# Two mixing steps with joined rows, moved from first and second to fifth and sixth place

## The chip, the cores and the metric

The kernel runs on one core of one Trainium2 chip, in one launch. The metric is the device time in microseconds (us). The profile is of one execution on that core; its engines are PE (matmul; PEld is the load of its weights), DVE (vector), ACT (scalar), POOL (GpSimd) and SP, which here only issues DMAs. Each engine works through its own queue of instructions in order.

## The reference

Four layers act on x of 4 images, 64 channels and 256 x 256 points. Layers 0, 2 and 3 are long convolutions with filters that a small network makes, separable in the two directions, plus x times a bias. Layer 1 is the one that concerns us: a two-dimensional Haar transform, for each of two filters a product with v, a mix of the 64 channels, a soft threshold, and the inverse transform of the sum.

```
f1 = haar2d(x)
acc = jnp.zeros_like(f1[:, :conv_w.shape[1]])
for i in range(v.shape[0]):
    f3 = f1 * v[i]
    f4 = jnp.einsum('bchw,oc->bohw', f3, conv_w[i])
    f5 = jnp.sign(f4) * jax.nn.relu(jnp.abs(f4) - tau[i])
    acc = acc + f5
y = haar2d(acc, inverse=True)
return y + x
```

## The kernel before

The four images are two groups of two. A *tile* of work is one group and one round (2 of the 64 channels); there are 32 rounds in a group. The convolutions are matmuls with Toeplitz matrices in float32.

**Phase A** (rows, columns, residual, then the forward Haar levels) goes through 64 tiles. Each has ten *pieces* j = 0 to 9, calls that record a few instructions: rows on PE with ACT copying the result (ay, L444), columns on PE with DVE adding the residual (x1, L464), sixteen forward steps on POOL (L344 and L346; the largest stand in pieces 0 and 1), the last Haar product on PE (a3ps, L308) with DVE scaling it (L477), and stores of the coefficients into the DRAM tensor coef of the group.

**Phase B** (`phase_b(grp)`, once for each group) mixes channels. It has 64 *steps* s; a step is four rows of points, with all 64 channels of the group's images on the partitions. Each step has two *units*, u = 2s and 2s + 1, one for each filter; so 128 units, of three pieces (u, 0), (u, 1), (u, 2). For one unit:

- `mix` (L607): eight matmuls of 64 x 64 into f4, which has one PSUM buffer; issued in the piece (u - 1, 1)
- `multiply` in (u, 0), DVE L626: x = f4 * v. `sign` in (u, 1), ACT L632: m. `magnitude` in (u, 2), ACT L641
- `less` in (u + 1, 0), DVE L646, and `threshold` in (u + 1, 1), DVE L651: subtract tau, cut at zero, times m
- `add` in (u + 2, 0), POOL L669 and L670 (first filter: plus the old coefficients f and `other`) or L666 (second filter), into gt
- `exchange` in (2s, 2), ACT L657: the tile `other`, a copy of half of f across the partitions
- `store` of gt into the DRAM tensor mixed, `load_f` and `load_v` for later steps, all on SP

Buffers in rings: ft 4, v 3, raw 3, m 3, gt 3, other 2, x 2, f4 1. A new tile takes the buffer of the tile so many places back, and its writer waits for the last reader of that one.

In group 1 (the last) the second filter of most steps is not thresholded here: DVE copies f4 to a tile raw (L623), which is stored in the DRAM tensor unshrunk, and phase C does the threshold later. Only the two *held* steps, those with the rows of the coarsest level, are done in full in phase B; for them the tile raw holds v and tau of the second filter, and zeros are stored in unshrunk (a memset on POOL, L681).

The forward transform leaves the coarsest level of the held steps unfinished: their rows have to be joined before mixing and parted after it. `join` (L575 to L586) is eight DVE operations on 64 x 256 for each of two images, in place in the two ft tiles, with a spare tile taken from the ring m; `part` (L588 to L599) is eight POOL operations on 64 x 512, in place in the two gt tiles, also with a spare from the ring m. The held steps are the first two, s = 0 and 1. All of join is one piece right ahead of `mix(0)`; all of part stands in the piece (6, 0), followed by the stores of both steps:

```
            if i == 0 and s == 3:
                part()
                store(0)
                store(1)
```

**Phase C** does the inverse transform and the last two convolutions for 64 tiles of 18 pieces: scales on ACT (L362), sixteen inverse steps on POOL (L385; the last two write ci) or DVE for the first two tiles (L387), the product c0ps on PE (L308), which reads ci and is copied to z by ACT or DVE (L849), then c1r, c1c, c2r, c2c on PE (L296) with their copies (ACT L861) and residuals (DVE L880), and stores of out. It reads the DRAM tensors mixed and unshrunk. Filters are loaded on SP (toep, L158), parts of g too (L758).

**The order** is written out by hand: `beside(main, side, lead, tail)` (L963) puts the pieces of side evenly between the pieces of main, and the instructions are recorded in that order for all engines. Phase B of group 0 runs beside the second half of phase A, about 1.5 side pieces to a main piece. Phase B of group 1 runs beside the first half of phase C, 0.8 side pieces to a main piece. In each, 13 pieces go ahead of piece (0, 0): `start` (which issues four `load_f` and three `load_v`), ten that do nothing, join, and `mix(0)`.

Of the kernel before, what the change touches and what calls it, by code (L numbers as in the profile page):

```python
# [41 lines left out]
F32 = mybir.dt.float32  # L42
AF = mybir.ActivationFunctionType
ALU = mybir.AluOpType
# [3 lines left out]
P = 128  # L48
B, C, N = 4, 64, 256
# [16 lines left out]
GROUPS = 2  # L66
NB = B // GROUPS
# [3 lines left out]
PAD = 128  # L71
# [2 lines left out]
HALVES = 2 * ROUNDS  # L74
STEPS = C
FULL = 2

A_PIECES = 2 * BLOCKS + 2
C_PIECES = 4 * BLOCKS + 2
# [2 lines left out]
W = 2 * N  # L82
# [16 lines left out]
def conv_haar_kernel(  # L99
    ctx: ExitStack, tc: tile.TileContext, x, zT, w1, wbd, cols, wo, decay, wo_first, decay_first, bias, forward, inverse, wrow, pack, v, v_rows, out  # L100
):
    nc = tc.nc
# [186 lines left out]
    def half(r):  # L289
        return slice(r * ROW, (r + 1) * ROW)  # L290
# [113 lines left out]
    def run(ops, count):  # L404
        for _ in range(count):
            next(ops, None)
# [117 lines left out]
    def phase_b(grp):  # L524

        units = 2 * STEPS
        mixers = []

        def raw(u):
            return grp == GROUPS - 1 and u % 2 == 1 and FULL <= u // 2 < STEPS  # L530
        st = [dict() for _ in range(STEPS)]
        un = [dict() for _ in range(units)]
        pieces = []

        def step_of(ap, s, images):

            n = NB * W
# [12 lines left out]
        def load_v(s):  # L550
            if s >= STEPS:
                return
            d = st[s]
            d["v"], d["tau"] = [], []

            def fetch(first, count, tag):
                n = 2 * count * W
                t = bp.tile([P, count, 2, W], F32, tag=tag, name=f"{tag}_{grp}_{first}_{s}", bufs=3)
                at = v.offset + s * P * (4 * W + PAD) + first * 2 * W
                rows = bass.AP(v.tensor, at, [[4 * W + PAD, P], [1, n]])  # L560
                nc.sync.dma_start(t.rearrange("p i k w -> p (i k w)"), rows)
                d["v"] += [t[:, i, 0] for i in range(count)]
                d["tau"] += [t[:, i, 1] for i in range(count)]
# [5 lines left out]
        def four(name, at, b):  # L569

            tiles = [st[s][name] for s in range(2)]
            tiles.append(bp.tile([P, NB, W], F32, tag="m", name=f"spare_{name}_{grp}_{b}", bufs=3))
            return [t[at, b, bass.ts(h, N)] for t in tiles for h in range(2)]

        def join(image):  # L575

            a, b, c, d, t, u = four("f", half(image), image)
            op = nc.vector.tensor_tensor
            op(t, a, b, ALU.add)
            op(b, a, b, ALU.subtract)  # L580
            op(u, c, d, ALU.add)
            op(d, c, d, ALU.subtract)
            nc.vector.tensor_scalar(c, b, math.sqrt(2.0), None, ALU.mult)
            nc.vector.tensor_scalar(d, d, math.sqrt(2.0), None, ALU.mult)
            op(a, t, u, ALU.add)
            op(b, t, u, ALU.subtract)  # L586

        def part():  # L588

            a, b, c, d, t, u = four("g", half(0), slice(0, NB))  # L590
            op = nc.gpsimd.tensor_tensor
            op(t, a, b, ALU.add)
            op(b, a, b, ALU.subtract)
            nc.gpsimd.tensor_scalar(u, c, math.sqrt(2.0), None, ALU.mult)
            op(a, t, u, ALU.add)
            nc.gpsimd.tensor_scalar(d, d, math.sqrt(2.0), None, ALU.mult)
            op(c, b, d, ALU.add)
            op(d, b, d, ALU.subtract)
            op(b, t, u, ALU.subtract)  # L599

        def mix(u):
            s, i = divmod(u, 2)
            un[u]["f4"] = bps.tile([P, NB, W], F32, tag="f4", name=f"f4_{grp}_{u}", bufs=1)
            for b in range(NB):
                for r in range(2):
                    q = r ^ b
                    nc.tensor.matmul(  # L607
                        un[u]["f4"][half(q), b, :],
                        mixers[0][half(r), bass.ts(i, C)],
                        st[s]["f"][half(r), b],  # L610
                        start=True,
                        stop=True,
                        tile_position=(r * ROW, q * ROW),
                    )
# [5 lines left out]
        def multiply(u):  # L620
            if raw(u):
                t = st[u // 2]["raw"] = bp.tile([P, NB, W], F32, tag="raw", name=f"raw_{grp}_{u}", bufs=3)
                nc.vector.tensor_copy(t, un[u]["f4"])  # L623
                return
            un[u]["x"] = bp.tile([P, NB, W], F32, tag="x", name=f"x_{grp}_{u}", bufs=2)
            nc.vector.tensor_tensor(un[u]["x"], un[u]["f4"], both(u, "v"), ALU.mult)  # L626

        def sign(u):
            if raw(u):
                return  # L630
            un[u]["m"] = bp.tile([P, NB, W], F32, tag="m", name=f"m_{grp}_{u}", bufs=3)
            nc.scalar.activation(un[u]["m"], un[u]["x"], AF.Sign)  # L632
# [20 lines left out]
        def exchange(s):  # L653

            st[s]["other"] = bp.tile([P, W], F32, tag="other", name=f"other_{grp}_{s}", bufs=2)
            for q in range(2):
                nc.scalar.copy(st[s]["other"][half(q)], st[s]["f"][half(1 - q), 1])  # L657

        def add(u):
            s, i = divmod(u, 2)  # L660
            if raw(u):
                un[u].clear()
                return
            m = un[u]["m"]
            if i:
                nc.gpsimd.tensor_tensor(st[s]["g"], st[s]["g"], m, ALU.add)  # L666
            else:
                g = st[s]["g"] = bp.tile([P, NB, W], F32, tag="gt", name=f"gt_{grp}_{s}", bufs=3)
                nc.gpsimd.tensor_tensor(g[:, 0], m[:, 0], st[s]["f"][:, 0], ALU.add)  # L669
                nc.gpsimd.tensor_tensor(g[:, 1], m[:, 1], st[s]["other"], ALU.add)  # L670
            un[u].clear()

        def store(s):
            to, g = step_of(mixed[grp], s, st[s]["g"])
            nc.sync.dma_start(to, g)
            st[s].clear()

        def store_raw(s):
            if s < FULL:
                t = st[s]["raw"] = bp.tile([P, NB, W], F32, tag="raw", name=f"none_{grp}_{s}", bufs=3)  # L680
                nc.gpsimd.memset(t, 0.0)  # L681
            to, g = step_of(unshrunk, s, st[s]["raw"])
# [301 lines left out]
    bp = pool("b", 2, during)  # L984
# [4 lines left out]
    a = a[-2 * A_PIECES :]  # L989
# [7 lines left out]
    bp = pool("b2", 2, during)  # L997
# [132 lines left out]
```

## Time and profile before

| what | us |
|---|---|
| median of three runs | 2571.49 |
| lowest, highest | 2568.22, 2571.54 |
| the profiled execution | 2557.88 |
| its span, first to last instruction | 2556.1 |
| PE busy in the span | 2314.9 (91%) |
| POOL busy | 2075.5 (81%) |
| DVE busy | 1835.7 (72%) |
| ACT busy | 1324.5 (52%) |

The shares are means over phases that differ. Group 0's mixing starts at about 429 us of the span (its first join operation), group 1's at 1133; the last multiply of group 1 is at 1841.5. In the page's 40 slices each slice is 63.9 us. In a line of the timeline the first number is the start, the second the time, and the bracket tells how long the engine had stood idle and which instruction released it. A line that begins with SPq is the issue of a DMA, not its transfer.

The operations that the change moves, from the answers for single lines (four executions of each line of join, two of each of part):

| line | engine | operation | ns min / median / max |
|---|---|---|---|
| L579 | DVE | tensor_tensor 64x256 | 422 / 441 / 593 |
| L581 | DVE | tensor_tensor 64x256 | 419 / 422 / 2556 |
| L583 | DVE | tensor_scalar 64x256 | 284 / 292 / 336 |
| L593 | POOL | tensor_tensor 64x512 | 1263 / 1270 / 1276 |
| L594 | POOL | tensor_scalar 64x512 | 1489 in both groups |
| L666 | POOL | add of the second filter | 2347 / 2362 / 2377 |
| L681 | POOL | memset | 943 / 948 / 954 |

### The profile page before, as it was taken

The page shows a single profiled execution, that of the slowest core. Times are in us where ns is not written, and L with a number is a line of the kernel's source. Part 1 is how long each engine was busy: PE and PEld are TensorE (multiplying, and loading weights), DVE is VectorE, ACT ScalarE, POOL GpSimd, SP SyncE. Part 2 cuts the span into 40 slices and gives each one's busy share as a digit, 9 for nine tenths or more (in the row PEclk, how much of TensorE's full clock was granted, in tenths as well). Part 3 has the DMA queues.
Part 4 walks back from the last instruction along what each step waited for, and adds up shares of the span by engine and source line. Part 5 has one row for each costly group of instructions (what it writes and reads, how often), then busy time and mean ns, then how long its engine had stood idle before and what let it go on. Part 6 is the DMA issues. An engine that isn't in the chain of part 4 may idle for free.

```text
span 2556.1 us, 118462 instructions
## 1 busy us (share of the span) xinstructions
PE 2314.9 (91%) x53292; PEld 1788.5 (70%) x53292; DVE 1835.7 (72%) x2049; ACT 1324.5 (52%) x2187; POOL 2075.5 (81%) x2428
## 2 busy tenths in 40 slices
PE   5999998788888888867999999999999999999999
PEld 4887787444444444646777877677788888888887
DVE  2555545799999999756677777767767777777763
ACT  1221212566666666325666666666656556556552
POOL 1898887889999999868768776766879999999990
PEclk8999999899999999989999999999999999999999
DMA  7676898699999999755989998889876666666643
GB/s 212 222 239 233 294 313 299 241 347 322 336 342 317 345 335 317 260 182 205 320 309 334 325 328 306 305 297 317 291 227 225 217 208 223 211 209 219 221 159 110
DMA packets 203677, 685.25 MB, mean 268 GB/s; under 512 B 29289, under 2 KB 30826, under 8 KB 190755
## 3 DMA queue, kind: packets, MB, share of 16 engines
q1 hardware_dynamic: 203171, 677.67, 77.3%
q8 instruction: 419, 6.86, 1.1%
q14 instruction: 87, 0.71, 0.1%
HBM read 427.93 MB, written 249.63 MB: 265 GB/s over the span
## 4 chain that ended last, share of the span: by engine, by line
PE 45%; DVE 5%; DMA 2%; issue 2%; ACT 2%; POOL 1%; SPq 0%; DVEq 0%; ACTq 0%; POOLq 0%
PE c2c L296 10%; PE c2r L296 10%; PE c1r L296 9%; PE c1c L296 8%; PE f L607 4%; PE c0ps L308 4%; DVE m L651 1%; DVE cy L880 1%; DVE x L646 1%; DVE x L626 1%; DMA g<-mixed 1%; ACT ch L861 0%; DMA toep<-filt 0%; DMA ft<-coef 0%; DMA rows<-in_v_rows 0%
## 5 line engine op out<-in xcount | busy, mean ns | idle before, releaser
L385 POOL TENSOR_TENSOR i<-i,g 128x16 f32<-128x16 f32 x744 | 437.3, 608 | 27.2
L296 PEld LDWEIGHTS a2ps<-toep,ay 64*64 64x64 f32 x8192 | 304.4, 136 | 143.4 <-DVE f L477 71.9
L607 PE MATMUL f<-ft,mix 64*64 64x512 f32 x2048 | 297.2, 619 | 117.7 <-DVE x L626 95.7
L296 PE MATMUL a2ps<-toep,ay 64*64 64x128 f32 (+3 forms) x8192 | 354.7, 305 | 30.5 <-DVE f L477 28.7
L296 PE MATMUL a1ps<-toep,x 64*64 64x64 f32 (+3 forms) x8192 | 340.7, 302 | 15.6 <-DMA x<-in_x 12.2
L296 PEld LDWEIGHTS a1ps<-toep,x 64*64 64x64 f32 x8192 | 292.1, 135 | 88.2 <-issue 43.2
L296 PEld LDWEIGHTS c2c<-toep,ch 64*64 64x64 f32 x8192 | 279.5, 134 | 72.5 <-issue 36.9
L296 PEld LDWEIGHTS c1c<-toep,ch 64*64 64x64 f32 x8192 | 275.9, 133 | 69.5 <-issue 38.3
L296 PE MATMUL c1r<-toep,z 64*64 64x64 f32 (+3 forms) x8192 | 309.8, 299 | 14.9 <-issue 9.9
L385 POOL TENSOR_TENSOR ci<-i,g 128x1024 f32<-128x1024 f32 x124 | 317.0, 2577 | 4.6
L296 PEld LDWEIGHTS c1r<-toep,z 64*64 64x64 f32 x8192 | 275.2, 135 | 60.7 <-issue 25.8
L444 ACT COPY ay<-a1ps 128x512 f32<-128x512 f32 x256 | 137.3, 589 | 347.0 <-PE a1ps L296 346.4
L632 ACT ACTIVATE m<-x 128x1024 f32<-128x1024 f32 x194 | 206.0, 1062 | 212.2 <-DVE x L626 104.5
L669 POOL TENSOR_TENSOR gt<-m,ft 128x512 f32<-128x512 f32 x128 | 163.4, 1277 | 181.1 <-DVE m L651 177.5
L296 PE MATMUL c2c<-toep,ch 64*64 64x128 f32 (+3 forms) x8192 | 306.7, 298 | 3.1 <-ACT ch L861 1.8
L296 PE MATMUL c2r<-toep,cy 64*64 64x192 f32 (+3 forms) x8192 | 302.8, 297 | 3.0 <-DMA toep<-filt 2.0
L296 PE MATMUL c1c<-toep,ch 64*64 64x128 f32 (+3 forms) x8192 | 301.0, 297 | 2.8 <-issue 2.8
L296 PEld LDWEIGHTS c2r<-toep,cy 64*64 64x64 f32 x8192 | 271.0, 134 | 46.0 <-issue 17.8
L861 ACT COPY ch<-c2r 128x512 f32<-128x512 f32 x256 | 137.4, 591 | 280.3 <-PE c2r L296 279.5
L477 DVE TENSOR_TENSOR f<-a3ps,wrow_sb 128x512 f32<-128x512 f32 x256 | 161.5, 682 | 133.0 <-PE a3ps L308 133.0
L626 DVE TENSOR_TENSOR x<-f,v 128x1024 f32<-128x1024 f32 x192 | 233.5, 1216 | 15.7 <-PE f L607 15.3
L880 DVE SCALAR_TENSOR_TENSOR o<-cy,bias_sb,c2c 128x512 f32<-128x512 f32 x256 | 176.7, 742 | 90.6 <-PE c2c L296 88.7
(84 smaller groups left out, 3917.6 us busy)
## 6 DMA issues: line engine op xcount, KB each, us to landing
toep<-filt SPq DMA_DIRECT2D x384, 224.0 KB, 5.3
ft<-coef SPq DMA_DIRECT2D x128, 512.0 KB, 7.5
v<-in_v SPq DMA_DIRECT2D x64, 1024.0 KB, 10.3
mixed<-gt SPq DMA_DIRECT2D x128, 512.0 KB, 6.8
g<-mixed SPq DMA_DIRECT2D x256, 256.0 KB, 5.2
x<-in_x SPq DMA_DIRECT2D x128, 256.0 KB, 4.4
coef<-f SPq DMA_DIRECT2D x128, 256.0 KB, 3.9
x<-in_x SPq DMA_DIRECT2D x32, 1024.0 KB, 8.3
```

The source lines that it names most:

```text
L296: nc.tensor.matmul(ps[r][half(c), j % 2, k * ROW :], data[half(r), c, k, bass.ts(j, ROW)], t(r, c)[:, : N - k * ROW], start=k == 0, stop=k ...
L308: nc.tensor.matmul(ps[r][half(c)].rearrange("p h k -> p (h k)"), matrix[half(r)], pairs(r, c).rearrange("p h k -> p (h k)"), start=True, s ...
L385: engine.tensor_tensor(to, s, d, op)
L444: later(lambda y=y, ps=ps: nc.scalar.copy(y, ps))
L477: later(lambda f=f, ps=ps, w=w: nc.vector.tensor_tensor(f, ps, w, ALU.mult))
L607: nc.tensor.matmul(un[u]["f4"][half(q), b, :], mixers[0][half(r), bass.ts(i, C)], st[s]["f"][half(r), b], start=True, stop=True, tile_posi ...
L626: nc.vector.tensor_tensor(un[u]["x"], un[u]["f4"], both(u, "v"), ALU.mult)
L632: nc.scalar.activation(un[u]["m"], un[u]["x"], AF.Sign)
L646: nc.vector.tensor_tensor(un[u]["a"], un[u]["a"], both(u, "tau"), ALU.subtract)
L669: nc.gpsimd.tensor_tensor(g[:, 0], m[:, 0], st[s]["f"][:, 0], ALU.add)
L861: later(lambda y=y, ps=ps: nc.scalar.copy(y, ps))
L880: nc.vector.scalar_tensor_tensor(to, of, bias_sb[:, at : at + 1], ps, ALU.mult, ALU.add)
```

## The change

The steps get an `order`: places 0 to 3 take the steps 2 to 5, places 4 and 5 the held steps 0 and 1, and from place 6 on each step is where it was. The kernel's s is now a place; `step_of` and the load of v look the step up.

- The piece of join is replaced by one that does nothing; it is still 13 pieces to piece (0, 0).
- join is a generator, four operations after each of the pieces (6, 0), (6, 1), (6, 2), (7, 0). Both images share a spare of one row, taken from the ring other instead of m.
- part is a generator, two operations after each of (13, 1), (13, 2), (14, 0), (14, 1). Its spare is from the ring m. The two stores come after (14, 2).
- The stores of the other early steps are no longer held back: in group 0 the places 0 to 3 are stored like later ones.
- In group 1 the units 1 and 3 become raw copies, and the units 9 and 11 get the full work of the second filter. The rows v and tau for it are loaded after (7, 2) and (9, 2) instead of with the first load_v. The memsets for unshrunk move along.

```diff
+LATE = 4
...
+        order = [*range(FULL, FULL + LATE), *range(FULL), *range(FULL + LATE, STEPS)]
+        held = range(LATE, LATE + FULL)
 
         def raw(u):
-            return grp == GROUPS - 1 and u % 2 == 1 and FULL <= u // 2 < STEPS
+            return grp == GROUPS - 1 and u % 2 == 1 and 0 < u < units and u // 2 not in held
...
-            fetch(0, 2 if grp < GROUPS - 1 else 1, "v")
-            if grp == GROUPS - 1 and not raw(2 * s + 1):
-                fetch(1, 1, "raw")
...
+        def join():
+
+            spare = bp.tile([P, 1, W], F32, tag="other", name=f"spare_f_{grp}", bufs=2)
             op = nc.vector.tensor_tensor
-            op(t, a, b, ALU.add)
...
+            for image in range(NB):
+                a, b, c, d, t, u = four("f", half(image), image, spare)
+                yield op(t, a, b, ALU.add)
...
         def part():
 
-            a, b, c, d, t, u = four("g", half(0), slice(0, NB))
+            spare = bp.tile([P, NB, W], F32, tag="m", name=f"spare_g_{grp}", bufs=3)
+            a, b, c, d, t, u = four("g", half(0), slice(0, NB), spare)
...
         def store_raw(s):
-            if s < FULL:
+            if s in held:
...
-                if i == 0 and s == 3:
-                    part()
-                    store(0)
-                    store(1)
-                if i == 0 and s > 3 and not raw(2 * s - 3):
+                if i == 0 and s > 1 and s - 2 not in held and not raw(2 * s - 3):
                     store(s - 2)
...
+                if i and s + 1 in held and grp == GROUPS - 1:
+                    fetch(s + 1, 1, 1, "raw")
+            if u == 2 * LATE - 2 and j == 0:
+                joining.append(join())
+            if u // 2 == LATE - 1:
+                run(joining[0], 4)
+            at = 3 * (u - 2 * (LATE + FULL) - 1) + j - 1
+            if at == 0:
+                joining.append(part())
+            if 0 <= at < 4:
+                run(joining[1], 2)
+            if at == 4:
+                for k in held:
+                    store(k)
...
-        pieces += [start] + [lambda: None] * 10 + [lambda: [join(b) for b in range(NB)], lambda: mix(0)]
+        joining = []
+        pieces += [start] + [lambda: None] * 11 + [lambda: mix(0)]
```

More of the change, by code (lines that the diff above doesn't have):

```diff
@@ L535, in step_of @@
         def step_of(ap, s, images):
-            n = NB * W
+            n, s = NB * W, order[s]
             at = ap.offset + s // 2 * PAIR + s % 2 * P // CI * n
@@ L552, in load_v @@
                 return
[L553 to L563, printed above, removed]
@@ L565, in load_v @@
-            fetch(0, 2 if grp < GROUPS - 1 else 1, "v")
-            if grp == GROUPS - 1 and not raw(2 * s + 1):
-                fetch(1, 1, "raw")
[L569 to L577, printed above, removed]
-            op = nc.vector.tensor_tensor
[L579 to L586, printed above, removed]
+            st[s]["v"], st[s]["tau"] = [], []
@@ new lines, in load_v, with fetch @@
+            fetch(s, 0, 2 if grp < GROUPS - 1 else 1, "v")
+        def fetch(s, first, count, tag):
+            d, n = st[s], 2 * count * W
+            t = bp.tile([P, count, 2, W], F32, tag=tag, name=f"{tag}_{grp}_{first}_{s}", bufs=3)
+            at = v.offset + order[s] * P * (4 * W + PAD) + first * 2 * W
+            rows = bass.AP(v.tensor, at, [[4 * W + PAD, P], [1, n]])
+            nc.sync.dma_start(t.rearrange("p i k w -> p (i k w)"), rows)
+            d["v"] += [t[:, i, 0] for i in range(count)]
+            d["tau"] += [t[:, i, 1] for i in range(count)]
@@ new lines, in four @@
+        def four(name, at, b, spare):
+            rows = [(st[s][name], b) for s in held] + [(spare, slice(0, spare.shape[1]) if b == slice(0, NB) else 0)]
+            return [t[at, b, bass.ts(h, N)] for t, b in rows for h in range(2)]
+        def join():
+            spare = bp.tile([P, 1, W], F32, tag="other", name=f"spare_f_{grp}", bufs=2)
+            op = nc.vector.tensor_tensor
+            for image in range(NB):
+                a, b, c, d, t, u = four("f", half(image), image, spare)
+                yield op(t, a, b, ALU.add)
+                yield op(b, a, b, ALU.subtract)
+                yield op(u, c, d, ALU.add)
+                yield op(d, c, d, ALU.subtract)
+                yield nc.vector.tensor_scalar(c, b, math.sqrt(2.0), None, ALU.mult)
+                yield nc.vector.tensor_scalar(d, d, math.sqrt(2.0), None, ALU.mult)
+                yield op(a, t, u, ALU.add)
+                yield op(b, t, u, ALU.subtract)
@@ L588, in part @@
         def part():
-            a, b, c, d, t, u = four("g", half(0), slice(0, NB))
+            spare = bp.tile([P, NB, W], F32, tag="m", name=f"spare_g_{grp}", bufs=3)
+            a, b, c, d, t, u = four("g", half(0), slice(0, NB), spare)
             op = nc.gpsimd.tensor_tensor
[L592 to L596, printed above, removed]
@@ L597, in part @@
-            op(c, b, d, ALU.add)
-            op(d, b, d, ALU.subtract)
-            op(b, t, u, ALU.subtract)
+            yield op(t, a, b, ALU.add)
+            yield op(b, a, b, ALU.subtract)
+            yield nc.gpsimd.tensor_scalar(u, c, math.sqrt(2.0), None, ALU.mult)
+            yield op(a, t, u, ALU.add)
+            yield nc.gpsimd.tensor_scalar(d, d, math.sqrt(2.0), None, ALU.mult)
+            yield op(c, b, d, ALU.add)
+            yield op(d, b, d, ALU.subtract)
+            yield op(b, t, u, ALU.subtract)
```

## The prediction

> **What bounds the kernel now.** I read the cores first (one core, clock 0.981), then a table of stretches chosen from the page's 40 slices, then the order of time around both starts of the mixing, and the chain of waits for the second. All times are of the profiled execution. It took 2557.88 us, 1.78 of it outside its span of 2556.1; the median of the three runs is 2571.49, so I forecast a difference and put it on both.
>
> ```profile
> core 0: us, PE busy (x) PEld busy (x) DVE busy (x) ACT busy (x) POOL busy (x), PEclk, DMA share, GB/s
> 463.00:497.80 34.80, 21.02 (x314) 13.98 (x312) 22.61 (x24) 14.74 (x18) 31.89 (x32) 0.85 0.46 164
> 497.80:521.30 23.50, 20.17 (x314) 12.93 (x312) 22.55 (x24) 15.88 (x20) 21.31 (x23) 0.93 1.02 410
> 521.30:1000.00 478.70, 388.20 (x6326) 228.45 (x6324) 457.67 (x466) 311.57 (x388) 434.94 (x477) 0.99 0.94 333
> 1130.00:1150.00 20.00, 9.95 (x93) 4.70 (x87) 10.02 (x17) 5.47 (x9) 7.13 (x6) 0.66 1.00 337
> 1150.00:1193.00 43.00, 39.84 (x958) 32.83 (x950) 35.92 (x32) 29.83 (x51) 35.68 (x29) 1.00 0.47 158
> 1193.00:1203.50 10.50, 0.47 (x8) 0.00 (x0) 3.42 (x2) 3.63 (x6) 10.34 (x7) 0.72 0.66 227
> 1300.00:1800.00 500.00, 473.13 (x11143) 388.47 (x11138) 362.79 (x345) 319.88 (x557) 368.75 (x410) 0.99 0.92 317
> ```
>
> Two regimes. Beside phase A (group 0, to about 1000) DVE sets the pace: 457.67 of 478.70 us, 96%, with POOL at 91%. Beside phase C (group 1) it is PE, 95%. A tile of phase A takes 23.5 us; the one from 463.0 takes 34.8 with the same DVE work, so it lost 11.3. PE did almost nothing from 1193 to 1203.5. Both holes are at part.
>
> ```profile
> 437.11 1.23 DVE L626 TENSOR_TENSOR x<-f,v 128x1024 f32<-128x1024 f32 x1 [2.06 <-PE f L607]
> 472.64 1.06 ACT L632 ACTIVATE m<-x 128x1024 f32<-128x1024 f32 x1 [6.47 <-POOL gt L670]
> 483.49 1.06 ACT L632 ACTIVATE m<-x 128x1024 f32<-128x1024 f32 x1 [6.50 <-POOL gt L599]
> ...
> 512.33 2.38 POOL L666 TENSOR_TENSOR gt<-gt,m 128x1024 f32<-128x1024 f32 x1
> 514.65 1.30 POOL L669 TENSOR_TENSOR gt<-m,ft 128x512 f32<-128x512 f32 x1
> 514.74 1.06 ACT L632 ACTIVATE m<-x 128x1024 f32<-128x1024 f32 x1 [0.81 <-POOL gt L666]
> ```
>
> Group 0: ACT's Sign cannot write its m until POOL has added the m whose buffer it takes (a ring of three). Part's spare tile takes one of the three, so twice ACT stood 6.5 us, and DVE behind it. An undisturbed tile waits 0.81 here: POOL's lag is at its limit in every tile.
>
> ```profile
> 1133.01 0.59 DVE L579 TENSOR_TENSOR spare_f<-ft 64x256 f32<-64x256 f32 x1 [8.87 <-DMA ft<-coef]
> 1139.18 1.98 PE L607 MATMUL f<-ft,mix 64*64 64x512 f32 x6 [7.16 <-DVE ft L586]
> 1146.01 2.84 PE L296 MATMUL c2r<-toep,cy 64*64 64x256 f32 x26 [1.95 <-DMA toep<-filt]
> 1193.99 1.27 POOL L599 TENSOR_TENSOR gt<-_slice(0, 2, None)_16305 64x512 f32<-64x512 f32 x1
> 1198.81 4.64 POOL L385 TENSOR_TENSOR ci<-i,g 128x1024 f32<-128x1024 f32 x2
> 1203.51 1.98 PE L308 MATMUL c0ps<-ci,inverse_sb 64*64 64x512 f32 x8 [10.04 <-POOL ci L385]
> ```
>
> Group 1: mixing waits for loads, then join; c2r waits for a filter load; part (1182.50 to 1195.26) delays ci, and PE waits 10.04 us for it.
>
> **What the Trainium skill says.** "Perfetto Trace Analysis", Per-engine timelines: ACT, DVE and GPSIMD are strict FIFO. The trace agrees: behind ACT's wait of 6.47, PE's a3ps waited 6.50 for an ACT copy. "GPSIMD Engine Reference", 1. Specifications: its SBUF interface is shared with DVE instructions that have two SBUF inputs. The trace agrees in part: one L581 took 2.56 us beside a ci of 2.41, its median is 0.42, but L646 keeps 1.23 throughout group 0. "TensorE: Matmul & The Clock Gate", Part 1: the clock halves after an idle window of about 3.4 us. It agrees: the eight c0ps at 1203.51 took 1.98, those at 1167.21 took 1.07.
>
> **The change, part by part.** The order of instructions on PE is the same in both kernels; those of the other engines keep their number and differ only near the two starts.
>
> *Start, group 0.* Join's 16 DVE operations (429.19 to 435.06, 5.9 us) leave. What is late next is v: the second of the three loads issued at 424.31 landed after 12.4 us, at 437.3. The first is 1 MB earlier; DMA moved 391 GB/s from 430 to 440, so 2.7 us earlier, 434.6. The first multiply moves from 437.11 to about there: gain 2.5 (0 if v0 is as late as v1, 5.9 if it isn't the limit).
>
> *Join, group 0.* The same 5.9 us now stand in units 6 and 7, where DVE is the bound. A normal tile has 1.0 us of DVE idle (23.50 less 22.55), which they fill: loss 5 (4 to 8). The one-row spare in "other" makes ACT's copy L657 of unit 6 wait for POOL's add of unit 4. Big forward steps precede that add on POOL by about 7 us, and the join holds DVE meanwhile, so I take 0; 3 if it isn't hidden. Behind it on ACT are the ay copies that PE's a3ps reads.
>
> *Part, group 0.* Two operations each after pieces (13,1), (13,2), (14,0), (14,1). On POOL that is: add 11, four operations, add 12, four, add 13. In the undisturbed tile add 11 ends at 514.7. Then four (1.26+1.26+1.49+1.26 and gaps, 5.4) to 520.1 and add 12 (2.6) to 522.7; sign 14, whose m is now that of add 12, goes from 514.74 to 522.7. Four more (5.5) and add 13 (2.4) end at 530.6; sign 15 follows, and DVE's L646 after its Abs is at 532.7 instead of 523.5: 9.2 late. That replaces 11.3: gain 2 (-3 to 11). SP stands at the two stores until the last operation (11 us for 20.1 before); behind them the x load for two tiles on.
> Group 0 in sum: 2.5 - 5 + 2 = -0.5, nothing.
>
> *Start, group 1.* Mixing no longer waits for join (7.16 + 0.93 on PE), but c2r at 1146.01 hangs on a filter load issued at 1134.23, in a stretch with DMA at 1.00. Two row loads of 512 KB ahead of it go to units 7 and 9: 1 MB at 337 to 415 GB/s is 2.5 to 3.1 us. Gain 2.5 (0 to 5). The new first unshrunk store waits on SP for a DVE copy, not a memset; behind it is a filter used some 25 us later: 0.
>
> *Join and second-filter work, group 1.* Eight of the 16 operations follow the multiply of unit 6, where DVE idles 3.36 us (ahead of 1183.99); the rest delay the multiply of unit 7 and, as f4 has one buffer, PE's next mix: loss 1.5 (0 to 6). Units 9 and 11 get Sign, Abs, two DVE operations, an add and a memset that units 1 and 3 had: DVE is at 73% there: 0.5. Their rows are fetched four pieces ahead, some 7 us (the multiplies from 1144.09 to 1841.5 are 126 units, 5.5 us for three pieces); such loads have a median landing of 6.9, 10.1 in the crowded start: loss 1.5 (0 to 8).
>
> *Part, group 1.* POOL loses 12.8 us of part and 6.6 of raw adds and memsets (2 x 2.36, 2 x 0.95) ahead of ci: ci would be ready near 1184, before PE asks at 1193.5. The wait of 10.04 goes, and with it the slow clock after it (c0ps and 96 c2c: 6.70 us against about 4.7): gain 12 (6 to 13). In its new place part stands among the first steps of an inverse whose ci is due about 14 main pieces later, and POOL is at 74%: loss 1 (0 to 10). SP's wait of 14.8 us before 1195.29, which held g loads that the chain of waits follows to 1215.8, shrinks; counted in the range.
> Group 1 in sum: 2.5 - 1.5 - 0.5 - 1.5 + 12 - 1 = 10.
>
> Together 9.5 us less: span 2546.6, this execution 2548.4, median 2562. Every later piece has its old neighbours and PE stays the bound to the end, so the shift should last.
>
> **Rivals.**
> *No change (2571, 2566.5 to 2576.5).* POOL still owes 12.8 us of part; if its idle in units 13 to 15 is short, c0ps waits again, or the DMA-bound start gives nothing. For: DMA shares of 0.90 and more from 1212. Against: POOL idles 5.03 us at once at 1234, near the new place.
> *Slower (2583).* Join's operations beside a busy POOL. Before, most ran while POOL idled (from 431 in group 0 and 1137 in group 1); now POOL is 73 to 91% busy. Each that meets a two-input POOL operation costs 2.1 more (2.56 - 0.42), on DVE in group 0 and through f4 in group 1. From 5 of 32 the gain is gone, from 8 it is measurably slower; at 10 it is 21 - 9.5 = +11.5. For: L580 and L581 at 1133.6. Against: L579 to L582 in group 0 ran at 0.42 to 0.46 beside small POOL steps.
> *Larger gain (2553).* Spread over four pieces, part in group 0 vanishes in POOL's idle (2.2 us a tile) and less lag: another 8 us. Against: the limit is met in each tile.
>
> **How the numbers follow.** Forecast 0.50, no change 0.21, slower 0.22, larger gain 0.07. Less than 0.2% (5 us) can't be told from no change. So faster 0.57, same 0.21, slower 0.22. The forecast's own range is 2556 to 2566.5. Adding most of the larger gain and the no-change case, and the near edge of the slower one, holds 0.8: 2550 to 2580.
>
> **What would show it.** Right: no c0ps wait on ci over 3 us near 1190; c2r near 1143.5; the first multiply of group 0 near 434.6; the tile with join near 28.5 us, the one with part near 32.7. Wrong: join operations of over 1 us, a multiply of unit 9 or 11 waiting for raw, c0ps waiting on POOL one or two tiles later, or a tile with part of 24 us.

## The result, and the profile after

The changed kernel takes 2582.82 us (median of ten runs, 2577.66 to 2587.88) against 2571.51 (2565.93 to 2576.19) of the kernel before in the same rounds. The ratio is 1.0041, with a 95% interval of 1.0027 to 1.0055: slower by 10.5 us. The forecast was 9.5 us less, so it was wrong in its direction and by 20 us; the time is almost exactly that of the rival named *Slower* (2583), though that rival's mechanism, join beside a busy POOL, makes up only some 9 of the 22 us by which the terms below miss.

The profiled execution took 2583.61 us. Its page, with the span and the busy time of the engines (share of the span, instructions):

```profile
span 2581.8 us, 118459 instructions
...
PE 2317.9 (90%) x53292; PEld 1870.3 (72%) x53292; DVE 1836.3 (71%) x2049; ACT 1324.5 (51%) x2187; POOL 2069.9 (80%) x2428
```

PE, DVE, ACT and POOL are as busy as before to within 6 us. The change made no work; it made waits. Lines have moved: join is now L580 to L587, part L594 to L601, multiply L628, the inverse steps L386. The list of PE's waits (us in total, times, longest):

```profile
PE f L609 <- DVE x L628: 103.2, 107, 9.1
...
PE c0ps L309 <- POOL ci L386: 11.3, 1, 11.3
...
PE c2r L297 <- DMA toep<-filt: 9.0, 1, 9.0
```

Before, the wait of c0ps for ci was 10.04, at 1203.51. The change removed that wait and made another of 11.3. The longest wait for a multiply was 2.4; it is 9.1 now. The table of stretches that answers to the one of before, with the tile of join, the tile of part, the old place of the hole, and the new one:

```profile
core 0: us, PE busy (x) PEld busy (x) DVE busy (x) ACT busy (x) POOL busy (x), PEclk, DMA share, GB/s
463.70:495.90 32.20, 20.70 (x314) 12.48 (x312) 31.95 (x40) 14.87 (x18) 23.36 (x24) 0.84 0.62 215
495.90:527.50 31.60, 21.70 (x342) 13.55 (x340) 24.74 (x25) 15.94 (x21) 30.69 (x31) 0.91 0.71 250
1193.00:1203.50 10.50, 8.52 (x114) 5.73 (x118) 7.55 (x11) 1.20 (x3) 5.03 (x10) 0.60 0.75 233
1255.50:1268.00 12.50, 1.17 (x39) 0.96 (x28) 2.18 (x2) 1.07 (x2) 12.34 (x10) 0.65 0.96 324
```

Group 0 had one long tile, of 34.8 us; now it has two, of 32.2 and 31.6. (A tile is taken from the issue of one load of x to that of the next.) In the first DVE is busy for 31.95 of 32.20 us (join), in the second POOL for 30.69 of 31.60 (part). In group 1 PE works again from 1193 to 1203.5, and is nearly idle from 1255.5 to 1268, with POOL busy for 12.34 of the 12.5.

To place the loss, I took the start of the multiply of each unit of group 1 in the kernel before, in the changed one, and in three experiments that are told below: the kernel before once more, the changed kernel without part, and the changed kernel with neither join nor part. Differences to the first profile of before, in us:

| unit | before | after | before again | after, no part | after, neither |
|---|---|---|---|---|---|
| 2 | 1154.68 | +3.3 | -0.5 | -9.6 | -15.0 |
| 6 | 1179.41 | -1.0 | -1.3 | -13.9 | -19.3 |
| 9 | 1193.54 | +11.9 | -1.3 | -2.6 | -16.0 |
| 10 | 1213.30 | -0.6 | -1.9 | -14.4 | -28.3 |
| 17 | 1252.66 | -0.6 | -0.4 | -14.3 | -28.2 |
| 24 | 1293.02 | +13.9 | -0.5 | -15.5 | -29.4 |
| 127 | 1843.95 | +21.2 | +9.0 | -8.7 | -19.8 |

Read down a column; where it jumps, something is won or lost. The changed kernel loses 12.9 between units 6 and 9 (mostly join), wins 12.4 at unit 10 (part's old place), and loses 14.5 between 17 and 24 (part's new place). The last jump goes where part is left out (1.2 won in both columns). Of the first, 3.3 stay in the last column, so they belong to neither join nor part. The last row is a caution: from unit 24 to 127 all the others in the table lose 7 to 10 us against the first profile of before, a second profile of the same kernel too. That one execution was quick there, so the spans, which differ by 25.7, overstate the loss.

### The profile page after: what moved, and what is told of

The parts are those of the page before. It is cut to its first block, busy times and chain, and to the rows that moved or that the text cites. A ratio compares the mean times of both kernels' runs of the same rounds, so it can differ in the third digit from the quotient of the medians.

```text
span 2581.8 us, 118459 instructions
## 1 busy us (share of the span) xinstructions
PE 2317.9 (90%) x53292; PEld 1870.3 (72%) x53292; DVE 1836.3 (71%) x2049; ACT 1324.5 (51%) x2187; POOL 2069.9 (80%) x2428
## 4 chain that ended last, share of the span: by engine, by line
PE 47%; DVE 4%; POOL 2%; issue 2%; ACT 1%; DMA 1%; SPq 0%; DVEq 0%; ACTq 0%; POOLq 0%
PE c2c L297 10%; PE c1r L297 10%; PE c2r L297 10%; PE c1c L297 9%; PE f L609 4%; PE c0ps L309 4%; DVE m L653 1%; POOL i L386 1%; DVE cy L893 1%; DVE x L628 1%; DVE x L648 0%; DMA toep<-filt 0%; DMA rows<-in_v_rows 0%; ACT ch L874 0%; DVE o L893 0%
## 5 line engine op out<-in xcount | busy, mean ns | idle before, releaser
L386 POOL TENSOR_TENSOR i<-i,g 128x16 f32<-128x16 f32 x744 | 434.1, 604 | 27.3
L609 PE MATMUL f<-ft,mix 64*64 64x512 f32 x2048 | 303.0, 624 | 117.8 <-DVE x L628 103.2
L297 PE MATMUL a2ps<-toep,ay 64*64 64x192 f32 (+3 forms) x8192 | 351.1, 304 | 30.0 <-DVE f L478 26.1
L297 PE MATMUL a1ps<-toep,x 64*64 64x64 f32 (+3 forms) x8192 | 338.9, 301 | 23.2 <-DMA x<-in_x 13.9
L297 PEld LDWEIGHTS c2c<-toep,ch 64*64 64x64 f32 x8192 | 305.5, 134 | 55.9 <-issue 28.8
L297 PEld LDWEIGHTS c1c<-toep,ch 64*64 64x64 f32 x8192 | 298.9, 133 | 45.5 <-issue 25.6
L297 PE MATMUL c1r<-toep,z 64*64 64x192 f32 (+3 forms) x8192 | 317.7, 300 | 15.4 <-issue 11.2
L297 PEld LDWEIGHTS c1r<-toep,z 64*64 64x64 f32 x8192 | 296.8, 135 | 46.0 <-issue 27.3
L297 PE MATMUL c2r<-toep,cy 64*64 64x128 f32 (+3 forms) x8192 | 310.1, 297 | 15.2 <-DMA toep<-filt 9.0
L297 PE MATMUL c2c<-toep,ch 64*64 64x64 f32 (+3 forms) x8192 | 313.1, 299 | 10.5 <-ACT ch L874 7.6
L297 PEld LDWEIGHTS c2r<-toep,cy 64*64 64x64 f32 x8192 | 293.7, 134 | 38.7 <-issue 17.0
L386 POOL TENSOR_TENSOR ci<-i,g 128x1024 f32<-128x1024 f32 x124 | 314.2, 2555 | 4.5
L297 PE MATMUL c1c<-toep,ch 64*64 64x192 f32 (+3 forms) x8192 | 305.5, 296 | 3.2 <-issue 2.0
L628 DVE TENSOR_TENSOR x<-f,v 128x1024 f32<-128x1024 f32 x192 | 233.5, 1216 | 33.9 <-DMA v<-in_v 21.3
```

The lines of the kernel that those rows point to most:

```text
L297: nc.tensor.matmul(ps[r][half(c), j % 2, k * ROW :], data[half(r), c, k, bass.ts(j, ROW)], t(r, c)[:, : N - k * ROW], start=k == 0, stop=k ...
L386: engine.tensor_tensor(to, s, d, op)
L609: nc.tensor.matmul(un[u]["f4"][half(q), b, :], mixers[0][half(r), bass.ts(i, C)], st[s]["f"][half(r), b], start=True, stop=True, tile_posi ...
```

## The experiments

All ratios are to the kernel before, in the same rounds.

**The kernel before again**, unchanged, one execution.

> The kernel before, unchanged, for one more profile of it. In the profiles at hand the kernel after lies 14 us behind at unit 24 of group 1 and 25.7 us behind at the end, while the medians differ by 11.3 us only. Theory 'lucky profile': the first profile of before (2557.88 us, median 2571.5) ran its second half unusually fast; then this one takes 2565 to 2577 us, its holes at part are as in the first (a tile of 34 to 35 us in group 0, a wait of c0ps for ci of 9 to 11 us in group 1), and its time from unit 24 of group 1 to the end is 7 to 14 us longer than in the first. Rival 'the change slows what comes later': that time is the first profile's within 3 us.

It took 2569.69 us, span 2567.7. Both holes are where they were (tile of 35.7, c0ps waiting 10.0). From unit 24 to the end of the span the first profile took 1263.1 us, this one 1275.2, and the changed kernel 1274.8. The tail is not a matter of the change.

**Part left out**, of the changed kernel and of the one before:

```diff
-                joining.append(part())
+                joining.append(iter(()))
```

```diff
-                    part()
                     store(0)
                     store(1)
```

> The kernel after without part's eight GpSimd operations and their spare, in both groups: the coarsest rows of the two held steps are left unparted. Theory 'part still costs a hole in each group': the tile of 31.6 us in group 0 becomes 23.5 to 24 (8 us), the wait of c0ps for ci of 11.34 us goes (12 us with the slow clock behind it): 17 to 22 us faster than after, ratio to before 0.995 to 0.998. Rival 'the later hole comes from the other GpSimd work that moved there (adds of units 9 and 11, memsets) and from the stall at join': c0ps still waits over 5 us, 8 to 12 us faster than after, ratio 0.999 to 1.002.

> The kernel before with the eight operations of part left out of both groups (mixed values of the first two steps stay unparted and are stored as they are; the stores keep their places). Theory: part costs about the same in the old place as in the new one, because in both it holds up GpSimd's queue once in each group (tile of 34.8 in group 0 against a steady 23.5; a wait of about 10 before the c0ps matmul in group 1): 20 to 24 us less than before, ratio 0.9907 to 0.9922, and neither hole left. Rival (part was cheap in its old place and the change made it dear): under 10 us less, ratio over 0.996.

**Join left out**, of the changed kernel and of the one before:

```diff
-                joining.append(join())
+                joining.append(iter(()))
```

```diff
-        pieces += [start] + [lambda: None] * 10 + [lambda: [join(b) for b in range(NB)], lambda: mix(0)]
+        pieces += [start] + [lambda: None] * 10 + [lambda: None, lambda: mix(0)]
```

> The kernel after without join's sixteen VectorE operations and their spare, in both groups: the coarsest rows are left unjoined. Theory 'join in its new place is on the path of both groups': the tile of 32.2 us in group 0 becomes 23.5 (8.7 us), the jump of 9 us at unit 7 of group 1 goes: 14 to 19 us faster than after, ratio to before 0.996 to 0.999. Rival 'join only shifts waits, what is gained is waited for at part': the wait of c0ps for ci grows by what unit 7 gains, 5 to 9 us faster than after, ratio 1.000 to 1.002.

> The kernel before with the sixteen operations of join left out of both groups (the first two steps are mixed unjoined). Theory: at the start of a group join stands beside the wait for the filter and sign loads, so it costs only what its start in the new kernel gained, about 2.5 us in each group: 3 to 6 us less than before, ratio 0.9977 to 0.9988, where leaving join out of the changed kernel was worth about 16 us. Rival (join costs the same wherever it stands): 14 us or more less, ratio under 0.995.

**Both left out of the changed kernel** (the two edits above together):

> The changed kernel with both join and part left out in both groups. It shows what the rest of the change is worth (new order of the loads, no join between the loads and the first mixing, second-filter work of the first steps of group 1). Theory: the costs add up: before without part is at 0.9912, and without join at 0.9988, so before with neither would be at 0.990; the changed kernel with neither starts group 0 2.4 and group 1 2.5 us earlier only because join is gone from the start, which leaving join out of before gives as well, so the two should be equal: 0.9885 to 0.991. Rival (the changed order of loads and the raw steps gain or lose something of their own): under 0.987 or over 0.993.

Measured:

| | kernel before | changed kernel |
|---|---|---|
| as it is | 1 | 1.0041 [1.0027, 1.0055] |
| no join | 0.9988 [0.9974, 1.0002] | 0.9980 [0.9968, 0.9991] |
| no part | 0.9912 [0.9887, 0.9937] | 0.9948 [0.9929, 0.9966] |
| neither | not run | 0.9892 [0.9870, 0.9915] |

Differences in a column, times 2571.5 us, are what the operations cost in that place. Part costs 22.6 us in its old place (1 - 0.9912) and 23.9 in the new one (1.0041 - 0.9948): about the same. Join costs 3 in its old place (an interval that touches nothing) and 15.7 in the new one. Each of the four has an uncertainty of 4 to 6 us. As far as they tell, the whole loss is join's, and part, whose holes the change seemed made to remove, paid nothing back. With neither, the changed kernel is at 0.9892; the sum for before is 0.9912 - 0.0012 = 0.9900, within the intervals, so the new order of loads and of second-filter work has no price of its own that intervals of some 6 us to either side can show. In group 0 the tiles of the changed kernel show it one by one:

| | tile of join | tile of part | the next |
|---|---|---|---|
| changed kernel | 32.17 | 31.63 | 24.58 |
| no part | 32.18 | 23.50 | 23.64 |
| no join | 23.66 | 31.63 | 24.58 |
| neither | 23.66 | 23.51 | 23.66 |

**Why join is dear in its new place.** In the timeline of the changed kernel, at join in group 0, DVE and POOL in order of their starts (start, duration, engine, line):

```profile
467.06 0.73 DVE L580 TENSOR_TENSOR spare_f<-ft 64x256 f32<-64x256 f32 x1
467.59 1.10 POOL L345 TENSOR_TENSOR fw<-f 128x512 f32<-128x512 f32 x1
467.83 1.15 DVE L581 TENSOR_TENSOR ft<-ft 64x256 f32<-64x256 f32 x1
468.66 1.21 POOL L347 TENSOR_TENSOR f<-f 128x512 f32<-128x512 f32 x1
468.90 1.25 DVE L582 TENSOR_TENSOR spare_f<-ft 64x256 f32<-64x256 f32 x1
...
472.56 1.30 POOL L672 TENSOR_TENSOR gt<-m,other 128x512 f32<-128x512 f32 x1
472.67 1.34 DVE L585 TENSOR_SCALAR ft<-ft 64x256 f32<-64x256 f32 x1
...
475.10 0.42 DVE L580 TENSOR_TENSOR spare_f<-ft 64x256 f32<-64x256 f32 x1
475.21 0.47 POOL L347 TENSOR_TENSOR f<-f 128x64 f32<-128x64 f32 x1
475.56 0.42 DVE L581 TENSOR_TENSOR ft<-ft 64x256 f32<-64x256 f32 x1
```

From L581 on each DVE operation shown beside a large POOL operation starts 0.1 to 0.3 us after it and ends 0.1 to 0.3 us after its end. L585, 0.29 alone, lasts 1.34 beside a POOL addition of 1.30. By 475, when POOL is at its small steps, the same operations are back at 0.42. In group 1:

```profile
1181.17 2.70 POOL L386 TENSOR_TENSOR i<-i,g 128x512 f32<-128x512 f32 x2
1183.95 4.88 POOL L386 TENSOR_TENSOR ci<-i,g 128x1024 f32<-128x1024 f32 x2
1185.34 1.26 DVE L582 TENSOR_TENSOR spare_f<-ft 64x256 f32<-64x256 f32 x1 [3.85 <-DMA ft<-coef]
1186.64 2.47 DVE L583 TENSOR_TENSOR ft<-ft 64x256 f32<-64x256 f32 x1
1189.14 0.28 DVE L584 TENSOR_SCALAR ft<-ft 64x256 f32<-64x256 f32 x1
...
1193.35 1.22 DVE L625 COPY raw<-f 128x1024 f32<-128x1024 f32 x1
```

Here two causes show: a wait of 3.85 for the coefficients of the second held step, which are loaded only one piece ahead of join, and 2.47 beside ci. At the last line unit 7 is 8 us late. The next run takes the load away, by issuing it four pieces earlier in group 1:

```diff
-                    if grp < GROUPS - 1:
+                    if grp < GROUPS - 1 or s == 2:
                         load_f(s + 3)
...
-                if i and s > 0 and grp == GROUPS - 1:
+                if i and s > 0 and s != 2 and grp == GROUPS - 1:
                     load_f(s + 3)
```

> The kernel after with the load of place 5 of group 1 issued four pieces earlier (after (4,1) instead of (5,2)). Theory 'the load was late': VectorE's wait of 3.85 us for it inside join goes and with it 3 to 5 us of the jump at unit 7, ratio to before 1.002 to 1.003. Rival 'the load is all of it': the whole jump of 9 us goes, ratio 1.000 to 1.001. Rival 'join's length beside GpSimd is all of it': unit 7 is as late as now, ratio 1.004.

The ratio is 1.0035 [1.0023, 1.0047]: no difference that these intervals can tell from the changed kernel's 1.0041. The timeline says why:

```profile
1183.00 1.39 DVE L583 TENSOR_TENSOR ft<-ft 64x256 f32<-64x256 f32 x1
1184.19 4.81 POOL L386 TENSOR_TENSOR ci<-i,g 128x1024 f32<-128x1024 f32 x2
1184.42 2.36 DVE L584 TENSOR_SCALAR ft<-ft 64x256 f32<-64x256 f32 x1
1186.71 2.45 DVE L585 TENSOR_SCALAR ft<-ft 64x256 f32<-64x256 f32 x1
1189.08 0.42 DVE L586 TENSOR_TENSOR ft<-spare_f 64x256 f32<-64x256 f32 x1
```

The load's wait is gone, and the operations wait for POOL in its stead: L584 and L585, 0.28 each in the run before, now take 2.36 and 2.45, one for each of the two ci steps. Join's first image ends at 1189.8 instead of 1190.3. DVE comes free when ci is done, whichever wait stands in front.

That is still a coincidence of lines, so the next run brings POOL work to a place where join was quick: in the kernel before, six additions on POOL are put beside join at each start.

```diff
+        def beside():
+            extra = bp.tile([P, NB, W], F32, tag="m", name=f"extra_{grp}", bufs=3)
+            for _ in range(6):
+                nc.gpsimd.tensor_tensor(extra, st[2]["f"], st[2]["f"], ALU.add)
...
-        pieces += [start] + [lambda: None] * 10 + [lambda: [join(b) for b in range(NB)], lambda: mix(0)]
+        pieces += [start] + [lambda: None] * 10 + [lambda: [beside(), *[join(b) for b in range(NB)]], lambda: mix(0)]
```

> The kernel before with six extra additions of a whole tile (128x1024, two SBUF operands) put on GpSimd beside join at the start of each group; their result is used by nothing. Theory (an operation of VectorE on SBUF operands is slow while a GpSimd operation on SBUF operands runs, whatever else is different about the place): join's operations, 0.28 to 0.42 each where GpSimd idled, become 1.2 to 2.6 while the six additions run, the tensor_scalar ones with one tensor operand too; join's sixteen span 12 us or more instead of 5.9, and each extra addition takes over its own 2.36. Rival (join is slow in its new place for another reason, such as VectorE's own queue or the shapes of the tiles): the operations keep 0.28 to 0.46, join spans 6 us. The time of the whole is not the point: 5 to 25 us more under the theory, since mixing starts later in both groups and GpSimd's queue is 14 us longer.

The timeline at the start of group 0:

```profile
434.91 0.41 DVE L585 TENSOR_TENSOR ft<-spare_f 64x256 f32<-64x256 f32 x1
435.01 12.24 POOL L736 TENSOR_TENSOR extra<-ft 128x1024 f32<-128x1024 f32 x6
435.25 2.10 DVE L586 TENSOR_TENSOR ft<-spare_f 64x256 f32<-64x256 f32 x1
437.38 2.00 DVE L579 TENSOR_TENSOR spare_f<-ft 64x256 f32<-64x256 f32 x1
...
445.53 1.87 DVE L583 TENSOR_SCALAR ft<-ft 64x256 f32<-64x256 f32 x1
447.32 0.28 DVE L584 TENSOR_SCALAR ft<-ft 64x256 f32<-64x256 f32 x1
```

In the same place, with the same operands, join's operations go from 0.42 to 2.00 and from 0.29 to 1.87 exactly while the additions run, and back. Six of the sixteen cost 10 us together: join spans 432.77 to 448.27, 15.5 us instead of 5.9. An addition has a median of 1.96, so one DVE operation waits for one addition. The additions themselves were expected above 2.36 and weren't. The kernel is at 1.0056 [1.0038, 1.0075], 14.4 us slower. This shows the mechanism away from join's new place: POOL work beside join is enough.

The Trainium skill states it: "SBUF — State Buffer", SBUF: two separate sides, calls the ports that VectorE and GpSimd share an exclusive lock, held for the whole instruction, with the other engine blocked; a VectorE operation takes part if it has two SBUF inputs (against a GpSimd operation that reads SBUF), or if it runs in a mode that uses two ports. The trace agrees: a blocked operation takes as long as the POOL instruction it meets (2.00 beside 1.96, 2.45 beside a ci of 2.4), not some factor longer.

**Can part leave POOL?** Four runs tried to take part, the larger cost, out of the queue that the holes hang on. All eight operations on DVE, in the changed kernel and in the one before:

```diff
-            op = nc.gpsimd.tensor_tensor
+            op = nc.vector.tensor_tensor
...
-            nc.gpsimd.tensor_scalar(u, c, math.sqrt(2.0), None, ALU.mult)
+            nc.vector.tensor_scalar(u, c, math.sqrt(2.0), None, ALU.mult)
```

> The changed kernel with the eight operations of part on VectorE instead of GpSimd, in the same pieces. Theory: GpSimd's queue is what part holds up; on VectorE eight operations of half the partitions by 512 take 5 to 10 us in each group, in fours of two operations over four pieces, so that the chain of GpSimd is no longer late: the wait of 11 us before c0ps goes, the tile of 31.6 in group 0 falls to 25 to 28, and the kernel is 8 to 16 us faster than the changed kernel, ratio to before 0.998 to 1.001. Rival (VectorE is the bound in this stretch too, and its operations slow down beside GpSimd's): within 5 us of the changed kernel, ratio 1.002 to 1.006.

> The kernel before with the eight operations of part on VectorE instead of GpSimd, all in one piece as before. Theory: the hole of 11.3 in group 0 falls to 4 to 7 and the c0ps wait of group 1 falls under 4, so 8 to 14 us less than before, ratio 0.9945 to 0.997, faster than both kernels. Rival: VectorE stands eight operations in a row and waits in them for GpSimd's last addition, so units behind it are late by the same 10 us: ratio 0.999 to 1.003.

The changed kernel with it is at 1.0023 [1.0010, 1.0035], the one before at 0.9974 [0.9961, 0.9987]. Both are faster than what they come from, by 4.6 us (the two intervals overlap) and 6.7 us, and both fall short of the 8 us that I expected at least; the first is in the range of its rival. The wait of c0ps for ci is gone in both. But in the changed kernel the third operation of part stood 2.43 us for a POOL addition, and what stood behind it on DVE with it; in the kernel before, DVE's operations took 1.3 to 2.7 beside POOL in group 1 (0.68 alone), and PE's longest wait for a multiply became 9.9. Its tile of part in group 0 fell only from 34.78 to 31.88. In the changed kernel that tile got longer, 34.11 instead of 31.63, where I had expected 25 to 28; POOL waited 7.51 us there for DVE.

Two of the eight operations on ScalarE, or six on DVE, four of them fused, both in the kernel before:

```diff
-            nc.gpsimd.tensor_scalar(u, c, math.sqrt(2.0), None, ALU.mult)
-            nc.gpsimd.tensor_scalar(d, d, math.sqrt(2.0), None, ALU.mult)
+            nc.scalar.mul(u, c, math.sqrt(2.0))
+            nc.scalar.mul(d, d, math.sqrt(2.0))
```

```diff
+            fused = nc.vector.scalar_tensor_tensor
             op(t, a, b, ALU.add)
-            op(b, a, b, ALU.subtract)
...
+            op(u, a, b, ALU.subtract)
+            fused(a, c, math.sqrt(2.0), t, ALU.mult, ALU.add)
+            fused(b, c, -math.sqrt(2.0), t, ALU.mult, ALU.add)
+            fused(c, d, math.sqrt(2.0), u, ALU.mult, ALU.add)
+            fused(d, d, -math.sqrt(2.0), u, ALU.mult, ALU.add)
```

> The kernel before with two of part's eight operations (the multiplications by the root of two) on ScalarE, ahead of the six left on GpSimd. Theory (each microsecond of part on GpSimd's queue is a microsecond of the two holes): the multiplications took 2.8 and 4.0 us on GpSimd in the two groups, so the holes of 11.3 and 12 shrink by about that: 5 to 7 us less than before, ratio 0.9973 to 0.998. Rival (the holes come from waits, not from the length of part): within 2 us of before, ratio 0.999 to 1.001.

> The kernel before with part on VectorE in six operations instead of eight (the multiplications by the root of two are fused into scalar_tensor_tensor). Part with eight operations on VectorE was 6.7 us faster than before; its operations took 0.68 alone and 1.3 to 2.7 beside GpSimd. Theory: two operations fewer save 1.4 to 4 us in each group where VectorE is late: 9 to 13 us less than before, ratio 0.995 to 0.9965, the fastest kernel of all. Rival: the fused operations take longer beside GpSimd than the two they replace, or VectorE isn't what is waited for: ratio 0.997 to 0.998 as with eight.

With two operations less on POOL, the tile of part is 32.41 (2.4 less) and the wait of c0ps 7.1 (2.9 less); the ratio is 0.9979 [0.9967, 0.9990], 5.4 us, as expected. The two multiplications had taken 3.0 us of POOL in group 0 and 3.9 in group 1: three quarters to four fifths of what leaves POOL's queue leaves the holes. Six operations on DVE give 0.9963 [0.9949, 0.9977], 9.5 us less than before: the lowest ratio of a version that does the whole work, though its interval overlaps those of the two above, and 20 us faster than the changed kernel. What is left in it is part's time on DVE, drawn out beside POOL (7.6 us for the six operations in group 0, 11.8 in group 1), in the waits of PE:

```profile
PE f L606 <- DVE x L625: 103.4, 113, 7.9
```

The longest of these was 2.4 in the kernel before: DVE holds a multiply up for as long as part stands in front of it.

## Why the prediction was wrong, term by term

| term | forecast, us | measured, us | from |
|---|---|---|---|
| Start, group 0 | -2.5 | -2.4 | tile 20.08 to 17.72 |
| Join, group 0 | +5 | +8.7 | tile 32.17 less 23.50 |
| Part, group 0 | -2 | -2.1 | 11.28 lost before; 8.13 + 1.08 now |
| Start, group 1 | -2.5 | -2.5 | issue of ft +5.8 late, c2r +3.3 |
| Join, second-filter work and fetch, group 1 | +3.5 | +8.6 | units 2 to 9 |
| Part, old place, group 1 | -12 | -12.4 | units 9 to 10 |
| Part, new place, group 1 | +1 | +14.5 | units 10 to 24 |
| sum | -9.5 | +12.4 | |

The measured terms are of one execution each. Their sum agrees with the 6.9 to 14.1 us of the ratio's interval, and with the 13.9 by which unit 24 is late. Four of the seven terms, all of what the change removes and the tile of part in group 0, were right to 0.4 us. The three wrong ones are of what it adds. (The first multiply of group 0 stood at 438.72 and not near 434.6 as forecast: this execution came into the stage 3.1 us later, so the multiply gained 1.5 and not 2.5, though the tile gained 2.4; v is still what it waits for.)

*Join, group 0: 5 taken, 8.7 found.* The sixteen operations were priced at the 5.9 us they took where POOL idled. The first eight took 7.2 us instead of 3.2, since the big forward steps of that tile were on POOL. That closes the sum: 5.9 and 4.0 more, less the 1.0 of idle time that they fill, is 8.9. (The copy that waits for the spare, put at 0, stood 0.80.) I had the mechanism at hand and argued it away: the trace "agrees in part", since "L646 keeps 1.23 throughout group 0". That was a misreading. In group 0 the operand a of L646 lies in PSUM, so the operation has one SBUF input and doesn't need the shared port: none of its 128 took over 1.233. In group 1, where x is in SBUF, the same line has a mean of 1.58 and takes up to 3.37, in the very trace that the forecast read; L648 of the changed kernel has 1.52. The exception was the rule.

*Join, group 1: 3.5 taken for the step, 8.6 found.* In the profile without join the same step loses 1.7 (unit 2 is 3.2 ahead of before, unit 9 only 1.5), so join is 6.9 of it, where 1.5 was taken. The rest, put at 2 for the second-filter work and its fetch, is 1.7. "DVE idles 3.36 us" there, and the forecast filled this with eight operations at 0.4; but two ci steps of 2.4 us each stood on POOL in just that time. The forecast had put them there itself: once part is gone, "ci would be ready near 1184".

*Part in its new place: 1 taken (0 to 10), 14.5 found.* This is the largest miss, and it decided the sign. The forecast found room in "POOL idles 5.03 us at once at 1234" and a ci "due about 14 main pieces later". In the changed kernel:

```profile
1236.14 2.37 POOL L668 TENSOR_TENSOR gt<-gt,m 128x1024 f32<-128x1024 f32 x1
...
1238.64 1.28 POOL L594 TENSOR_TENSOR spare_g<-gt 64x512 f32<-64x512 f32 x1
...
1252.80 1.26 POOL L601 TENSOR_TENSOR gt<-spare_g 64x512 f32<-64x512 f32 x1
1254.03 6.87 POOL L386 TENSOR_TENSOR i<-i,g 128x128 f32<-128x128 f32 x6
...
1263.30 4.65 POOL L386 TENSOR_TENSOR ci<-i,g 128x1024 f32<-128x1024 f32 x2
...
1268.00 1.98 PE L309 MATMUL c0ps<-ci,inverse_sb 64*64 64x512 f32 x8 [11.34 <-POOL ci L386]
```

POOL has no idle time from 1213.5 to 1272: the 5.03 us were gone before part came. They had been idle time of the old order. The forecast credited 6.6 us for the second-filter additions and memsets that the change takes from ahead of the old ci, and didn't charge them where they went, ahead of the new one. The changed kernel with neither join nor part shows these alone:

```profile
1208.53 2.37 POOL L668 TENSOR_TENSOR gt<-gt,m 128x1024 f32<-128x1024 f32 x1
...
1224.29 5.67 POOL L386 TENSOR_TENSOR ci<-i,g 128x1024 f32<-128x1024 f32 x2
1230.01 1.09 PE L309 MATMUL c0ps<-ci,inverse_sb 64*64 64x512 f32 x8 [0.67 <-POOL ci L386]
...
1256.04 1.04 PE L309 MATMUL c0ps<-ci,inverse_sb 64*64 64x512 f32 x8
...
1281.39 1.07 PE L309 MATMUL c0ps<-ci,inverse_sb 64*64 64x512 f32 x8
```

There POOL runs without a gap from 1191 to 1239, and c0ps already waits 0.67 us for this ci. (Part of the lost idle time is the port again: three additions of 128x512 between 1202 and 1216, beside DVE operations, take 2.27 to 2.31 there, 1.27 elsewhere.) The slack was zero, so part's eight operations (10.6 us, 10.8 with the gaps between) came on top of it and made a wait of 11.34. That the new place is as dear as the old is partly chance. In the kernel before without part, the ci at the old place is ready 4.5 us ahead of PE (at 1179.25, for c0ps at 1183.75). In the lines above, the next two ci, ready at 1251.54 and 1273.56, are 4.5 and 7.8 us ahead. The new place had the least slack of all these. No run put part further back.

*The rivals.* "Slower" named the right place for join, and its threshold of 5 to 8 blocked operations was passed (eleven, at 0.2 to 2.1 us more each). Its time of 2583 agrees by chance: it took 21 us for join and still counted the gain of 12 from part. "No change" held the other half: "c0ps waits again" is what happened, with a price of 11 instead of some 5. The two were weighed as alternatives, and both came true. Of the signs that were to show the forecast wrong, two appeared: join operations of over 1 us, and c0ps waiting on POOL one or two tiles later.

What stays open: where the 3 us come from that the loss between units 17 and 24 has beyond the 11.3 of the wait. They are absent without part, and they shrink to 1.4 without join, where this stretch loses 11.1 with a wait of 9.74. They stand beside a slow clock (0.65 in the hole), but no run takes them apart.

## What to carry to other kernels

Where two engines share a port, the price of an operation is that of its neighbours: before moving VectorE work with two SBUF inputs, or a float32 tensor_scalar from SBUF to SBUF, list what GpSimd runs in the new place, and count the length of one GpSimd instruction for each that meets. Idle time read from the old trace belongs to the old order: what the change itself moves has to be put into the new place first, and only then is it seen what room is left. And in a queue that another engine waits for, a place is priced by the slack of the next delivery, read in the new order: here it was nothing at the place that was taken, and 4.5 and 7.8 us at the next two. Whether one of those would have been cheaper for part was not measured; that it gets cheaper when it is made shorter or leaves the queue was, by 5 to 10 us in the kernel before.

## What the runs showed of the hardware

Either side can be the one that waits. Beside the six extra additions (1.93 to 2.07 us each; what one takes alone was not measured) each DVE operation but one waited out one addition. Beside part's six operations on DVE in group 0, POOL's additions of 128x512 took 1.71 us instead of 1.27, and the DVE operations 0.98 to 1.64; a plain one takes 0.68 alone, and what a fused one takes alone was not measured. A DVE multiplication with a single tensor operand in float32 (L583) is held up like those with two, 1.87 instead of 0.29, as that run's expectation had it.
